# Attention and channel mixing on one core: how the first batch's q and k rows reach their tiles, and what TensorE does meanwhile

## The chip, the cores and the metric

The kernel runs on one core of a Trainium2 chip. TensorE (PE) multiplies, VectorE (DVE) copies and reduces, ScalarE (ACT) computes Exp and Ln, GpSimd (POOL) works on SBUF, SyncE (SP) issues DMAs. ACT and POOL can issue DMAs as well. The metric is the device time of one execution in microseconds; the time before is the median of three runs, 1013.5 us (1011.57 to 1015.29).

## The reference

The input x is [16, 512, 128] in float32. With 16 heads, q and k of 8 columns a head and v of 64, the reference computes

```
xn   = layernorm(x)                                    # no affine part
q, k = xn @ Wq, xn @ Wk ;  v = xn @ Wv                 # 16 heads
attn = softmax(causal(q @ k.T / sqrt(8))) @ v @ Wo
prev = xn shifted by one row
xr, xk = mu_r*xn + (1-mu_r)*prev, mu_k*xn + (1-mu_k)*prev
ffn  = sigmoid(xr @ W_r.T) * (relu(xk @ W_k.T)**2 @ W_v.T)
out  = x + attn + ffn
```

## The kernel before

Each batch element is one batch of 20 units. A unit belongs to a group g of two head pairs (four groups a batch) and has a kind t of 0 to 4; `ROWS` and `KEYS` say which 128-row blocks of which pair it covers.

Softmax is done twice over. First `rowscores` computes scores with rows on partitions into one of two `sm` tiles in PSUM, `rowmask` adds the causal mask as a matmul, `rowmax` reduces on DVE (negm<-sm), and `rowsum` takes Exp on ACT with a running sum (sm<-sm,negm). After a group's five units `log_sums` takes Ln, `sub_logs` subtracts, `turn_stats` transposes the result on PE (pm) and splits it into mh and ml, and `put_stats` writes them as two extra rows into the q tile by DMAs from POOL (q<-mh, q<-ml). Then `scores` computes the transposed scores with these rows included (sT<-q,k), so that one Exp (`weights`, e<-sT) gives the final softmax weights. `weigh` multiplies them with v (av), `project_out` applies Wo (po).

The first half runs `LEAD` = 10 units ahead of the second. `unit_work(n)` issues rowscores of unit n+11, scores of unit n, the mask and maximum of n+11, rowsum of unit n+10, `weights` of n, then the pieces that `at(n, f, ...)` has registered for this n, and last turn_stats. Units -11 to -1 are called the lead here: they have no second half. Every engine works in the written order (`_InOrder`); an instruction that waits holds all behind it on its engine.

float32 q and k are split into two float32r parts, hi and lo, so that the scores can run in the faster form. A tile `qs[i]` or `ks[i]` holds, for each of the eight pairs, 32 rows per head (q: hi, lo, hi, lo; k: hi, lo, lo, hi; 8 rows each), one row of ones or zeros and two rows for the statistics; u picks one head of the pair, at partition 64u. The projection leaves hi and lo with (d, head) on partitions, so `project_qk` writes them to DRAM (q two blocks, k three) and `spread_qk` reads them back, 16 rows per DMA, in the new layout. For batch 0 the spreads come in three steps, pairs 0 and 1, 2 and 3, and 4 to 7 (lines 624 to 626 and 647 to 648). The writes of k of batch 0 and its first spreads go through ACT's queue, all others through SP's.

Until unit -1, `m_tile` hands out PSUM tiles in turn from three banks (m, av, sT); a projection needs its bank's last reader to be done. `product` is two matmuls side by side, each for 64 columns; the trace counts two instructions for each.

Before the lead the kernel loads x of batches 0 and 1 and the weights, computes batch 0's layernorm, transposes xn (xnTp), projects q and k, prepares the masks, turns the three ffn weights on PE (wt), then does the layernorm, the transpose and q of batch 1 (lines 638 to 644). Inside the lead come k of batch 1, all eight v products of batch 0 (two of its halves for each of four row blocks, copied out by DVE), the mixes and ffn_r.

Of the kernel before, what the change touches and what calls it, by code (L numbers as in the profile page):

```python
# [17 lines left out]
P = 128  # L18
# [31 lines left out]
def attn_ffn_kernel(  # L50
# [66 lines left out]
    ffn_n = []  # L117
    for i, w in enumerate((W_r, W_k, W_v)):
        t = one.tile([P, D], FP, tag=f"ffn_n{i}", name=f"ffn_n{i}")
        nc.scalar.dma_start(out=t, in_=w)  # L120
        ffn_n.append(t)
    wo = const.tile([P, NPAIR, D], FP, tag="wo", name="wo")
    nc.scalar.dma_start(out=wo, in_=Wo.rearrange("(m p) d -> p m d", p=P))
# [28 lines left out]
    def m_tile(name):  # L152
        n = lent[0] % 3 if lent else 0
        if lent:
            lent[0] += 1
        if n == 1:
            return ps_av.tile([P, T], FP, tag="av", name=name)
        if n == 2:
            return ps_st.tile([P, 2, 512], FP, tag="sT", name=name)[:, 0, :]
        return ps_m.tile([P, 512], FP, tag="m", name=name)  # L160

# [56 lines left out]
    def project_qk(b, is_k, queue=sp):  # L218

        w, name = (wk, "k") if is_k else (wq, "q")  # L220
        pq = m_tile(f"p{name}_{b}")
        product(pq, w, xnTs[b][:, 1 : T + 1])
        hi = one.tile([P, T], FR, tag=f"{name}h", name=f"{name}h_{b}")
        lo = one.tile([P, T], FR, tag=f"{name}l", name=f"{name}l_{b}")
        dve.tensor_copy(hi, pq)
        dve.tensor_tensor(lo, pq, hi.bitcast(FP), ALU.subtract)

        blocks = (hi, lo, hi) if is_k else (hi, lo)
        d = dram.tile([len(blocks), P, T], FP, tag=name, name=f"{name}_{b}")
        for n, half in enumerate(blocks):  # L230
            queue.dma_start(out=d[n], in_=half.bitcast(FP))
        halves[b, name] = d.rearrange("n (d p u) t -> u (n d) p t", u=2, d=DK)

    def spread_qk(b, is_k, m, u, pairs, queue=sp):

        to, name = ((ks if is_k else qs)[b % 2].bitcast(FP), "k" if is_k else "q")
        first = DK * m if is_k else 0
        queue.dma_start(
            out=to[64 * u + 16 * m : 64 * u + 16 * m + 16, pairs],
            in_=halves[b, name][u][first : first + 16, pairs],  # L240
        )
# [3 lines left out]
    def project_v(b, j, i):  # L245
# [4 lines left out]
        dve.tensor_copy(vs[b][:, j, i * 512 : (i + 1) * 512], pv)  # L250
# [341 lines left out]
    make_qk(0)  # L592
    for c in range(NB):
        row_moments(0, c)
# [4 lines left out]
    project_qk(0, False)  # L599
    project_qk(0, True, act)  # L600
# [23 lines left out]
    for pairs in (slice(0, 2), slice(2, 4)):  # L624
        for is_k, m, u in SPREAD:
            spread_qk(0, is_k, m, u, pairs, act if is_k and pairs.stop == 2 else sp)

    ffn_w = const.tile([P, 3, D], FP, tag="ffn_w", name="ffn_w")
    wt = m_tile("wt")
    for i in range(3):  # L630
        pe.transpose(wt[:, i * D : (i + 1) * D], ffn_n[i], ident)
    dve.tensor_copy(ffn_w.rearrange("p i d -> p (i d)"), wt[:, 0 : 3 * D])

# [3 lines left out]
    load_x(2)  # L637
    for c in range(NB):
        row_moments(1, c)
    deviation(1)  # L640
    for c in range(NB):
        normalise(1, c, dve)
    transpose_xn(1)
    project_qk(1, False)
    first = -LEAD
    at(first + 1, project_qk, 1, True)
    for m, part in enumerate(SPREAD):
        at(first + 2 + m // 2, spread_qk, 0, *part, slice(4, NPAIR))
    for m, n in enumerate((0, 2, 3, 4, 5, 6, 7, 9)):
        at(first + n, project_v, 0, m // 2, m % 2)  # L650
    for i in range(2):
        at(first - 1 + 5 * i, mix_prev, 0, i)
        at(first + 1 + 6 * i, mix, 0, i)
# [47 lines left out]
```

## Time and profile before

| what | value |
|---|---|
| median of the runs | 1013.5 us |
| the profiled execution's own time | 1015.34 us |
| span of its trace | 1013.6 us |
| busy: PE, ACT, DVE, POOL | 949.4, 921.6, 790.4, 512.4 us |
| first softmax Exp on ACT | 29.41 us |
| first Exp of transposed scores | 58.39 us |
| mean granted TensorE clock | 0.975 |

The profile follows one execution. Busy time is the union of an engine's instructions; a granted clock of 1.00 is full, 0.50 is half speed. A group's row gives the line, the engine, the operation, the tiles out<-in, and the count. The chain of waits is followed back from the last instruction: each piece is what released the next. Queue rows (SPq, ACTq) show when a DMA was issued, not when it landed. Nearly every instruction stands under one helper line (L44), so rows are told apart by their tiles.

### The profile page before, as it was taken

The numbers are of one execution on the slowest core, as the hardware profiler recorded it, in microseconds if no ns is written. First come the engines' busy times: TensorE is split into PE (matmuls) and PEld (weight loads), VectorE is DVE, ScalarE is ACT, GpSimd is POOL, SyncE is SP. The second block draws the span as 40 slices with busy tenths as digits, with TensorE's granted clock in tenths as the row PEclk, the third lists the DMA queues.
The fourth block names the chain that finished last, engine by engine and source line by source line (L and its number), as shares of the span: only waits on it lengthen the run. The fifth ranks groups of instructions, "written<-read, shape, count | busy, mean of one in ns | idle before, by whom it ended". The sixth has DMA issues, their size and how long they took to land.

```text
span 1013.6 us, 22825 instructions
## 1 busy us (share of the span) xinstructions
PE 949.4 (94%) x8131; PEld 524.4 (52%) x8131; DVE 790.4 (78%) x1312; ACT 921.6 (91%) x2449; POOL 512.4 (51%) x959
## 2 busy tenths in 40 slices
PE   3888999999999999999999999999999999999997
PEld 1244464555546455554645555464555646455454
DVE  4777878787887878788787878878787887877641
ACT  0688999999999999999999999999999999999982
POOL 4146364554646455454645555464465546434431
PEclk8578999999999999999999999999999999999999
DMA  8730513535142353514235341423534131343000
GB/s 183 134 45 13 110 19 70 91 70 91 34 101 28 70 91 70 90 34 99 31 70 90 70 91 34 96 34 70 90 71 81 33 95 25 70 80 49 3 13 11
DMA packets 59968, 67.10 MB, mean 66 GB/s; under 512 B 12928, under 2 KB 33024, under 8 KB 59856
## 3 DMA queue, kind: packets, MB, share of 16 engines
q1 hardware_dynamic: 48688, 61.89, 32.4%
q10 hardware_dynamic: 2528, 2.43, 1.0%
q0 software_dynamic: 8640, 1.34, 1.0%
q8 instruction: 65, 1.06, 0.5%
q14 instruction: 47, 0.39, 0.1%
HBM read 39.13 MB, written 25.17 MB: 63 GB/s over the span
## 4 chain that ended last, share of the span: by engine, by line
ACT 55%; PE 27%; issue 8%; DVE 7%; DMA 2%; POOL 1%; ACTq 0%; POOLq 0%
ACT sm L44 37%; ACT e L44 17%; PE av L44 9%; PE po L44 5%; DVE negm L44 4%; PE sm L44 4%; PE pv L44 3%; PE sT L44 3%; PE xnTp L44 1%; PE pr L44 1%; DVE xnT L44 1%; DMA q<-ml 1%; DVE v L44 1%; DMA k<-k 1%; PE pk L44 1%
## 5 line engine op out<-in xcount | busy, mean ns | idle before, releaser
L44 ACT ACTIVATE sm<-sm,negm 128x384 f32<-128x384 f32 (+3 forms) x1024 | 513.0, 501 | 64.9 <-DMA k<-k 27.3
L44 DVE TENSOR_REDUCE negm<-sm 128x2 f32<-128x768 f32 (+3 forms) x448 | 397.9, 912 | 101.3 <-PE sm L44 99.2
L44 POOL TENSOR_SCALAR_AFFINE_SELECT e<-e 128x256 f32<-128x256 f32 x512 | 200.5, 410 | 432.4 <-ACT e L44 432.3
L44 PE MATMUL av<-e,v 128*64 128x512 f32 (+3 forms) x2048 | 336.5, 438 | 2.4 <-DVE ctx L44 2.4
L44 ACT ACTIVATE e<-sT 128x1024 f32<-128x1024 f32 x320 | 324.1, 1013 | 14.1 <-PE sT L44 14.1
L44 PEld LDWEIGHTS av<-e,v 128*64 128x64 f32 x2048 | 139.7, 137 | 161.6 <-issue 129.6
L44 ACT ACTIVATION_READ_ACCUMULATOR sm<-sm,negm 128x1 f32 x1024 | 200.5, 196 | 0.0
L44 PE MATMUL sm<-k,q 33*128 33x384 f32 (+3 forms) x1024 | 164.8, 378 | 7.4 <-ACT sm L44 5.4
L44 PE MATMUL sT<-q,k 35*128 35x512 f32 (+3 forms) x1024 | 147.7, 335 | 16.5 <-ACT e L44 13.0
L44 PEld LDWEIGHTS sm<-k,q 33*128 33x128 f32 x1024 | 83.6, 188 | 151.8 <-ACT e L44 82.0
L44 PE MATMUL pv<-wv,xnT 128*64 128x512 f32 x512 | 142.3, 633 | 12.6 <-DVE kl L44 5.8
L44 PE MATMUL po<-wo,ctx 128*64 128x128 f32 x2048 | 133.2, 277 | 2.9 <-DVE ctx L44 1.6
L44 PEld LDWEIGHTS po<-wo,ctx 128*64 128x64 f32 x2048 | 109.8, 137 | 15.4 <-DVE v L44 2.6
L44 PEld LDWEIGHTS sT<-q,k 35*128 35x128 f32 x1024 | 91.2, 187 | 45.9 <-ACT e L44 40.0
L44 DVE COPY v<-pv 128x512 f32<-128x512 f32 x128 | 87.6, 684 | 23.2 <-PE pv L44 19.7
L44 DVE COPY ctx<-av 128x512 f32<-128x512 f32 x128 | 87.1, 680 | 12.7 <-PE av L44 12.6
L44 PE MATMUL sm<-mask,id 64*128 64x256 bf16 (+1 forms) x640 | 91.0, 265 | 0.0
L44 POOL DMA_DIRECT2D q<-mh x128 | 69.8, 548 | 24.9 <-DVE mh L44 12.8
L44 POOL DMA_DIRECT2D q<-ml x128 | 65.8, 519 | 0.0
L44 DVE RECIPROCAL sig<-e_sig 128x128 f32<-128x128 f32 x64 | 60.1, 940 | 0.0
L44 POOL TENSOR_SCALAR prev<-xnT,omm 128x512 f32<-128x512 f32 x32 | 50.0, 1564 | 16.2 <-DVE xmix L44 16.2
L44 PEld LDWEIGHTS <-id 64*128 64x128 bf16 x640 | 36.3, 95 | 24.8 <-issue 10.5
(63 smaller groups left out, 571.1 us busy)
## 6 DMA issues: line engine op xcount, KB each, us to landing
q<-q SPq DMA_DIRECT2D x124, 128.0 KB, 4.9
k<-k SPq DMA_DIRECT2D x124, 128.0 KB, 4.7
k<-kh SPq DMA_DIRECT2D x30, 256.0 KB, 2.6
x<-in_L_attn_x_dram SPq DMA_DIRECT2D x16, 256.0 KB, 6.5
q<-qh SPq DMA_DIRECT2D x16, 256.0 KB, 2.0
q<-ql SPq DMA_DIRECT2D x16, 256.0 KB, 2.1
out_dram<-o SPq DMA_DIRECT2D x16, 256.0 KB, 2.8
k<-kl SPq DMA_DIRECT2D x15, 256.0 KB, 2.0
```

The lines of the kernel that those rows point to most:

```text
L44: return self._tc.keep_in_program_order(f(*args, **kwargs))
```

## The change

Five things change, all before or inside the lead.

1. `keep_awake(n)` issues n transposes of the identity into one `m_tile` that nobody reads: 32 after `make_qk(0)`, 4 between the transpose of xn and the projection of q.
2. For pairs 0 and 1 of batch 0 the rows are no longer read back from DRAM. `spread_near` copies them from the hi and lo tiles in SBUF straight into the q and k tiles, 8 partitions of 2 KB per DMA, 16 DMAs on SP for q and 16 on ACT for k, issued ahead of the writes to DRAM. The writes all go through SP now; pairs 2 to 7 still come from DRAM.
3. The first five v products of batch 0 are issued right after k, ahead of the first rowscores, and copied out by ACT. Three remain in the lead, at units -9, -8 and -3.
4. The layernorm of batch 1, its transpose and its q move into the lead, k to a later unit of it; its normalise runs on POOL, not on DVE.
5. The ffn weights are loaded by SP after the projections and turned inside the lead; Wo is loaded at unit -3, x of batch 2 at unit -5. The two mixes of batch 0 move by a few units.

```diff
--- before.py
+++ after.py
@@ -114,13 +114,6 @@
         wqk_n.append(t)
     wv = const.tile([P, H * DV], FP, tag="wv", name="wv")
     nc.scalar.dma_start(out=wv, in_=Wv)
-    ffn_n = []
-    for i, w in enumerate((W_r, W_k, W_v)):
-        t = one.tile([P, D], FP, tag=f"ffn_n{i}", name=f"ffn_n{i}")
-        nc.scalar.dma_start(out=t, in_=w)
-        ffn_n.append(t)
-    wo = const.tile([P, NPAIR, D], FP, tag="wo", name="wo")
-    nc.scalar.dma_start(out=wo, in_=Wo.rearrange("(m p) d -> p m d", p=P))
     if B > 1:
         load_x(1)
     mus = const.tile([P, 2], FP, tag="mus", name="mus")
@@ -158,6 +151,12 @@
         if n == 2:
             return ps_st.tile([P, 2, 512], FP, tag="sT", name=name)[:, 0, :]
         return ps_m.tile([P, 512], FP, tag="m", name=name)
+
+    def keep_awake(n):
+
+        pt = m_tile("awake")
+        for c in range(n):
+            pe.transpose(pt[:, (c % NB) * P : (c % NB + 1) * P], ident, ident)
 
     xnTs, vs, ctxs, ffns, xmix = {}, {}, {}, {}, {}
 
@@ -215,7 +214,7 @@
         dve.tensor_copy(xnT[:, 1 : T + 1], pt)
         xnTs[b] = xnT
 
-    def project_qk(b, is_k, queue=sp):
+    def project_qk(b, is_k, first=None):
 
         w, name = (wk, "k") if is_k else (wq, "q")
         pq = m_tile(f"p{name}_{b}")
@@ -227,27 +226,38 @@
 
         blocks = (hi, lo, hi) if is_k else (hi, lo)
         d = dram.tile([len(blocks), P, T], FP, tag=name, name=f"{name}_{b}")
+        if first:
+            first(hi, lo)
         for n, half in enumerate(blocks):
-            queue.dma_start(out=d[n], in_=half.bitcast(FP))
+            sp.dma_start(out=d[n], in_=half.bitcast(FP))
         halves[b, name] = d.rearrange("n (d p u) t -> u (n d) p t", u=2, d=DK)
 
-    def spread_qk(b, is_k, m, u, pairs, queue=sp):
+    def spread_near(is_k, p, half, n, queue):
+
+        to = (ks if is_k else qs)[0].bitcast(FP)
+        half = half.bitcast(FP).rearrange("(d h) t -> h d t", d=DK)
+        for m in ((0, 3), (1, 2))[n] if is_k else (n, n + 2):
+            for u in range(2):
+                row = 64 * u + DK * m
+                queue.dma_start(out=to[row : row + DK, p], in_=half[2 * p + u])
+
+    def spread_qk(b, is_k, m, u, pairs):
 
         to, name = ((ks if is_k else qs)[b % 2].bitcast(FP), "k" if is_k else "q")
         first = DK * m if is_k else 0
-        queue.dma_start(
+        sp.dma_start(
             out=to[64 * u + 16 * m : 64 * u + 16 * m + 16, pairs],
             in_=halves[b, name][u][first : first + 16, pairs],
         )
 
     SPREAD = [(is_k, m, u) for m in range(2) for is_k in (False, True) for u in range(2)]
 
-    def project_v(b, j, i):
+    def project_v(b, j, i, copy=dve.tensor_copy):
         if j == 0 and i == 0:
             vs[b] = big.tile([P, NB, H * DV], FP, tag="v", name=f"v_{b}")
         pv = m_tile(f"pv_{b}_{j}_{i}")
         product(pv, xnTs[b][:, 1 + j * P : 1 + (j + 1) * P], wv[:, i * 512 : (i + 1) * 512])
-        dve.tensor_copy(vs[b][:, j, i * 512 : (i + 1) * 512], pv)
+        copy(vs[b][:, j, i * 512 : (i + 1) * 512], pv)
 
     def mix_prev(b, i):
         prev = one.tile([P, T], FP, tag="prev", name=f"prev_{b}_{i}")
@@ -590,14 +600,18 @@
 
 
     make_qk(0)
+    keep_awake(32)
     for c in range(NB):
         row_moments(0, c)
     deviation(0)
     for c in range(NB):
         normalise(0, c, dve)
     transpose_xn(0)
-    project_qk(0, False)
-    project_qk(0, True, act)
+    keep_awake(4)
+    project_qk(0, False, lambda *both: [spread_near(False, p, half, n, sp) for p in range(2) for n, half in enumerate(both)])
+    project_qk(0, True, lambda *both: [spread_near(True, p, half, n, act) for p in range(2) for n, half in enumerate(both)])
+    for m in range(5):
+        project_v(0, m // 2, m % 2, act.copy)
 
 
 
@@ -621,36 +635,48 @@
             dve.tensor_copy(to[half], wide[half, i, P * u : P * u + P])
 
     make_qk(1)
-    for pairs in (slice(0, 2), slice(2, 4)):
-        for is_k, m, u in SPREAD:
-            spread_qk(0, is_k, m, u, pairs, act if is_k and pairs.stop == 2 else sp)
-
-    ffn_w = const.tile([P, 3, D], FP, tag="ffn_w", name="ffn_w")
-    wt = m_tile("wt")
-    for i in range(3):
-        pe.transpose(wt[:, i * D : (i + 1) * D], ffn_n[i], ident)
-    dve.tensor_copy(ffn_w.rearrange("p i d -> p (i d)"), wt[:, 0 : 3 * D])
-
+    ffn_n = []
+    for i, w in enumerate((W_r, W_k, W_v)):
+        t = one.tile([P, D], FP, tag=f"ffn_n{i}", name=f"ffn_n{i}")
+        sp.dma_start(out=t, in_=w)
+        ffn_n.append(t)
+    for part in SPREAD:
+        spread_qk(0, *part, slice(2, 4))
 
     omm = const.tile([P, 2], FP, tag="omm", name="omm")
     dve.tensor_scalar(omm, mus, -1.0, 1.0, ALU.mult, ALU.add)
-    load_x(2)
+
+    ffn_w = const.tile([P, 3, D], FP, tag="ffn_w", name="ffn_w")
+    wo = const.tile([P, NPAIR, D], FP, tag="wo", name="wo")
+
+    def turn_ffn():
+        wt = m_tile("wt")
+        for i in range(3):
+            pe.transpose(wt[:, i * D : (i + 1) * D], ffn_n[i], ident)
+        dve.tensor_copy(ffn_w.rearrange("p i d -> p (i d)"), wt[:, 0 : 3 * D])
+
+    def load_wo():
+        sp.dma_start(out=wo, in_=Wo.rearrange("(m p) d -> p m d", p=P))
+
+    first = -LEAD
     for c in range(NB):
-        row_moments(1, c)
-    deviation(1)
+        at(first - 1 + c // 2, row_moments, 1, c)
+    at(first + 1, deviation, 1)
     for c in range(NB):
-        normalise(1, c, dve)
-    transpose_xn(1)
-    project_qk(1, False)
-    first = -LEAD
-    at(first + 1, project_qk, 1, True)
+        at(first + 1 + c // 2, normalise, 1, c)
+    at(first + 3, transpose_xn, 1)
+    at(first + 4, project_qk, 1, False)
+    at(first + 5, turn_ffn)
+    at(first + 6, project_qk, 1, True)
+    at(first + 5, load_x, 2)
+    at(first + 7, load_wo)
     for m, part in enumerate(SPREAD):
         at(first + 2 + m // 2, spread_qk, 0, *part, slice(4, NPAIR))
-    for m, n in enumerate((0, 2, 3, 4, 5, 6, 7, 9)):
+    for m, n in ((5, 1), (6, 2), (7, 7)):
         at(first + n, project_v, 0, m // 2, m % 2)
     for i in range(2):
-        at(first - 1 + 5 * i, mix_prev, 0, i)
-        at(first + 1 + 6 * i, mix, 0, i)
+        at(first + 2 + 4 * i, mix_prev, 0, i)
+        at(first + 4 + 4 * i, mix, 0, i)
     at(first + 8, ffn_r, 0)
     at(first + 9, ffn_exp, 0)
     for c, n in enumerate((1, 2, 3, 3)):
```

## The prediction

> **What bounds the kernel now.** I read the clock and busy rows of the page first, then a table of stages, then the chain of waits and the timeline of the first 60 us.
>
> ```profile
> PE   3888999999999999999999999999999999999997
> ACT  0688999999999999999999999999999999999982
> PEclk8578999999999999999999999999999999999999
> ```
>
> After the third slice (76 us) PE and ACT are full in every slice. The page's slices are too coarse for the start, so I cut it where ACT's work changes: first softmax Exp at 29.41, first Exp of transposed scores (e) at 58.39, twentieth unit after it at 125.16, and one whole batch. Columns: stretch, length, PE, PEld, DVE, ACT, POOL, granted clock, DMA share, GB/s.
>
> ```profile
> 2.07:29.41 27.34, 11.67 (x37) 4.49 (x37) 14.30 (x45) 0.00 (x1) 10.68 (x20) 0.77 0.94 195
> 29.41:58.39 28.98, 24.10 (x107) 8.41 (x103) 21.30 (x31) 22.62 (x76) 5.22 (x6) 0.68 0.84 128
> 58.39:125.16 66.77, 59.84 (x405) 29.22 (x406) 54.25 (x87) 58.19 (x154) 36.22 (x62) 0.87 0.21 45
> 125.16:184.47 59.31, 57.62 (x511) 32.40 (x508) 48.81 (x82) 57.35 (x154) 31.82 (x59) 1.00 0.34 67
> ```
>
> A batch costs 59.31 us with ACT busy 57.35, and the change leaves that alone. To be won are ACT's 27.34 us of idleness before its first Exp (A), 28.98 - 22.62 = 6.4 us idle in the lead (B), and 66.77 - 59.31 = 7.5 us in the first twenty units (C). The chain says who holds ACT in A and B:
>
> ```profile
> 13.96 0.70 DVE kh L44
> 14.69 0.70 DVE kl L44
> 15.41 4.88 DMA k<-kl
> ...
> 21.62 5.02 DMA k<-k
> 26.66 2.77 DMA k<-k
> 29.43 0.67 ACT sm L44 x2
> ...
> 32.85 1.90 PE pk L44 x4
> ...
> 35.61 1.90 PE pv L44 x4
> ...
> 48.36 8.96 DMA q<-ml
> 57.32 0.14 issue
> 57.46 0.57 PE sT L44 x2
> ```
>
> In A it is the trip of k through DRAM: 15.41 to 29.43, 14 us. In B it is PE at half clock, with projections between the scores, then q<-ml (the row statistics put into q), which lands as the first e is due. Two rows show what the clock is worth and one how SP issues:
>
> ```profile
> 44.03 1.97 PE L44 MATMUL pv<-wv,xnT 128*64 128x512 f32 x4
> 49.00 1.08 PE L44 MATMUL pv<-wv,xnT 128*64 128x512 f32 x4
> 44.99 1.33 SPq L44 DMA_DIRECT2D q<-q  x2
> ```
>
> The same product takes 1.97 us before 47.8 and 1.08 after. SP issues only two DMAs per 2.05 us there (42.94, 44.99, 47.04): each names one of eight semaphores in turn, shared with ACT, and waits until the DMA eight before it has landed.
>
> **The change, stage A.** Thirty-two transposes of the identity start at 1.85, when POOL has made it. Two transposes of xn stand 0.213 us apart at half clock, so they end by 8.7; xn's first is due at 8.33 but its last waits for DVE until 9.09: at most 0.2 us late, taken as 0. Four more (0.44 to 0.85) fall into PE's 0.79 us gap before pq: 0.
>
> Do these transposes lift the clock? No row shows transposes alone. In 10.25 to 13.67 PE streamed pq and pk for 3.32 of 3.42 us, and at 13.84 three transposes came 0.11 apart, at full clock. By that row 6.8 us of back-to-back transposes do it too; pq and pk then take 1.06 each instead of 1.90, and kl is ready at about 14.3, not 15.38. If not, A is 1.1 later. I take the lift, with 1.1 kept for the range.
>
> One rule speaks against it: the Trainium skill, TensorE: Matmul & The Clock Gate, section on the PE-mode transpose, says transposes do not count as PE activity and full clock does not engage for them. By it the sum would be 1010.1, against 1009.0; no run here shows which holds.
>
> The row copies replace the DRAM trip. For pairs 0 and 1, q's halves go in 16 DMAs on SP (from 12.2), k's in 16 on ACT (from 13.6), 8 partitions and 16 KB each. ACT and SP issue the old 64 KB spreads 0.33 to 0.45 apart: alone, ACT would be through at 13.6 + 16 x 0.44 = 20.6, at 0.33 at 18.9. With eight in flight and the shortest spread's 2.06 us to landing plus a little, one leaves per 0.275; 32 plus q's two writes of 256 KB take 34 x 0.275 = 9.4, so 21.6. The other end is the spacing at which the contended 64 KB spreads landed, 0.53: 34 x 0.53 = 18, so 30.2. A near DMA has a quarter of those bytes and the eight-partition form of the statistics DMAs, which landed in 1.6 at best; I take 21.0.
>
> This delay matters, because the five early v products stand on PE ahead of the first rowscores, and ACT copies them out behind its 16 issues. Three PSUM banks rotate: pv0 to pv2 run by about 15.5, pv3 waits for ACT's first copy. A copy is costed at the 0.65 of ACT's 128x512 Exp: pv3 starts at 21.7. PE has then idled 6 us; after 13.67 it worked 0.72 in 3.41 and the clock fell at 17.08. So pv3 and pv4 cost 1.90 each, to 25.5; rowscores and mask 1.03 (31.82 to 32.85), the two reductions 1.3: first Exp at 27.9, a gain of 1.5. At the ends: 18.9 + 0.65 + 2.1 + 0.7 + 1.3 = 23.7, and 30.2 + 6.9 = 37.1. The copies add 5 x 0.65 to ACT where it is idle; a table load, should Copy need its own, would add 1.28 twice, but Exp and Ln share one, so 0.
>
> SP is passed by 16 issues ahead of the q and k writes, so d is full later, near 25, and pairs 2 and 3 land about 33; they are due at the sixth unit, about 38. The ffn weights moved to SP (three, 64 KB) and wo are due after 40: 0. DVE's 5 x 0.69 of v copies leave it.
>
> **Stage B.** Off PE: five v products, 9.5 us at half clock. Onto it: four transposes 0.85, pq 1.90, wt 0.55; net -6.2. DVE: -3.45, and xnT 0.69, q's halves 1.38, ffn_w 0.56, batch 1's moments 1.4: +0.6. POOL takes the normalise, 4 x 0.79 and the 1.05 of rstd, into a stage where it is busy 5.22 of 28.98: 0; without cover unit -7's transposes hold PE for up to 1.
>
> What remains is the two sm buffers: unit m+2's scores wait for ACT's end of unit m, then need 1.03 on PE, 1.24 on DVE, and hand-offs, about 2.4, while ACT fills only 1.6 with a unit of two 512-wide rows. That is 0.8 at four units, 3.2; with full clock 0.45 each. I keep 1.8 of today's other stalls, since fewer products still stand between scores on PE and DVE is as full: 22.6 + 5.0 = 27.6, gain 1.4. Ends: 22.6 + 1.8 = 24.4; today's plus DVE's, 29.6.
>
> The first e comes at 27.9 + 27.6 = 55.5. It also needs q<-ml: lz came 12.8 after the first Exp, POOL's first issue 5.1 after that, its second pair 1.1 later, 8.96 to landing: 55.8. Queued around it now are k's 768 KB and wo's 512 KB, while batch 1's spreads, which ran ahead there, wait behind them; undisturbed it took 1.6. On the edge: 0.
>
> **Stage C.** No instruction in it changes. Two half-clock spells lie in it, 58.04 to 68.28 and 88.76 to 95.58; the chain's PE pieces in them (sT 0.79, pk 1.90, av 1.71, sm 0.72, sT 0.43; then sT 0.86, pv 1.90, av 2.56) would halve, 2.8 and 2.7. The first followed PE's idling for q<-ml (1.21 busy in 54.62 to 58.04). I count about half of one: 1.6; ends +5.5 and, with one more such spell, -2.7.
>
> **Sum.** 1.5 + 1.4 + 1.6 = 4.5 us. The profiled execution took 1015.3 (span 1013.6 and 1.7 around it), 1.8 above the median of 1013.5; it becomes 1010.8, and on the median 1009.0.
>
> **Rivals.** *Small DMAs clog (slower).* ACT sits behind its 16 issues, PE behind pv3. For: the spreads landed 0.53 apart, eight in flight. Against: a quarter of the bytes. From 0.36 us per DMA on, A eats B's and C's gains; at 0.5 it ends at 36.1: +6.7 - 3.0, 1017.2.
>
> *Statistics take it back (no change).* q<-ml needs 12 instead of 9 because of wo and k: first e at 58.8, PE idles, the clock falls, A and B gain nothing: 1013. Against: the spreads that crowded it are later.
>
> *The clock holds (more).* Sustained PE work from pv3 on lifts it for the lead: A 25.5, B 24.4, C 62: 3.9 + 4.6 + 4.8 = 13.3, 1000.2. For: pv3 to the second unit's scores are 5.5 us without a gap. Against: 34.15 to 47.8 was nearly gapless on PE and stayed at half clock.
>
> **How the numbers follow.** Forecast 0.50 (own range 1005 to 1013), clock 0.18, statistics 0.20, clog 0.12. 0.3% is 3.0 us, about what a measurement of this kernel can tell. Faster: 0.40 of the forecast, all 0.18, 0.02 of the statistics: 0.60. Slower: 0.09 of the clog and 0.03 of the statistics: 0.12. Same: 0.28. The range 1002.0 to 1016.0 leaves out about half of the clock case and half of the clog.
>
> **What would show it.** Transposes 0.11 apart before 8 us: the lift. ACT's last near issue at 21.0 and pv3 right after ACT's first copy: the wait I add. First Exp at 27.9, first e at 55.5, twentieth unit at 120.7. pv in the lead at 1.97: half clock. It is wrong if near DMAs leave faster than 0.2 or slower than 0.36 apart, if pv3 does not wait for ACT, or if batches after the second no longer take 59.3.

## The result and the profile after

The changed kernel takes 1018.7 us (median of six executions, 1016.03 to 1020.12) against 1012.8 for the kernel before (six executions, 1009.48 to 1015.29): a ratio of 1.0058, 95% interval 1.0035 to 1.0082. It is slower by 5.9 us where 4.5 faster was forecast. The profiled execution took 1016.03 us (span 1014.3).

The page's rows for PE, ACT and the granted clock, in 40 slices, look as before: only the first four slices differ.

```profile
PE   4788999999999999999999999999999999999997
ACT  0688999999999999999999999999999999999982
PEclk8769999999999999999999999999999999999999
```

The table of stages of the changed kernel, cut at the same events as before (first softmax Exp at 32.81, first e at 61.15, twentieth unit after it at 125.61, one batch). Columns: stretch, length, busy time and count of PE, PEld, DVE, ACT and POOL, granted clock, DMA share, GB/s.

```profile
2.07:32.81 30.74, 16.86 (x78) 9.21 (x77) 8.64 (x28) 2.74 (x6) 7.98 (x17) 0.78 0.51 136
32.81:61.15 28.34, 21.73 (x99) 9.48 (x99) 23.16 (x42) 22.57 (x76) 10.99 (x13) 0.65 0.66 143
61.15:125.61 64.46, 57.40 (x403) 28.48 (x405) 52.68 (x85) 58.24 (x154) 36.26 (x62) 0.92 0.30 59
125.61:184.95 59.34, 57.60 (x511) 32.40 (x508) 49.05 (x82) 57.41 (x155) 31.79 (x59) 1.00 0.37 67
```

A batch still costs 59.3. The clock of stage A is too high in both tables: the profile counts the time ahead of its first clock record as full. That record begins at 6.91 here, and until then the transposes stood 0.213 apart, 0.11 after it. Stage A is longer by 3.4 us, although its DMA share fell from 0.94 to 0.51: the engines that move data are no longer what it waits for. The timeline of the stage shows what is. Columns: start, busy time, engine (SPq and ACTq are DMA issues), operation, tiles, count, and in brackets the idle time before it with what ended it.

```profile
12.02 3.72 SPq L44 DMA_DIRECT2D q<-qh  x4
13.35 4.39 ACTq L44 DMA_DIRECT2D k<-kh  x4
15.85 3.53 SPq L44 DMA_DIRECT2D q<-ql  x4
17.84 2.64 ACTq L44 DMA_DIRECT2D k<-kl  x4
...
20.52 2.92 ACTq L44 DMA_DIRECT2D k<-kh  x4
...
23.48 2.92 ACTq L44 DMA_DIRECT2D k<-kl  x4
...
26.45 1.56 ACT L44 COPY v<-pv 128x512 f32<-128x512 f32 x3 [24.38 <-DMA k<-kl]
...
27.09 3.68 PE L44 MATMUL pv<-wv,xnT 128*64 128x512 f32 x8 [11.81 <-ACT v L44]
...
30.70 0.54 PE L44 MATMUL sm<-k,q 33*128 33x384 f32 x4
...
32.81 0.56 ACT L44 ACTIVATE sm<-sm,negm 128x384 f32<-128x384 f32 x1 [1.42 <-DVE negm L44]
```

ACT issues its sixteen near copies from 13.35 to 26.40; four take 2.92 there, 0.73 each. Its first copy of v starts at 26.45, and PE, idle for 11.81 us, starts the fourth v product when ACT's copy is out. The bracket names a DMA, but ACT's own queue ended at 26.40 (23.48 + 2.92): the copy came right behind the last issue. From there it is the chain that the prediction wrote down, 6.4 us long, only 5.4 us late.

Two windows of the same execution, 12.0 to 17.2 and 17.2 to 24.0, same columns, say the rest:

```profile
12.00:17.20 5.20, 3.03 (x14) 0.54 (x10) 2.77 (x8) 0.00 (x0) 0.00 (x0) 1.00 0.37 40
17.20:24.00 6.80, 0.00 (x0) 0.00 (x0) 0.00 (x0) 0.00 (x0) 0.00 (x0) 0.50 0.12 40
```

In the second, no engine computes anything and the DMA engines are 12% busy, with the copies that SP and ACT issue.

Each kernel was traced three times. Stages, in us:

| | A, to first Exp | B, to first e | C, twenty units | end of C |
|---|---|---|---|---|
| before | 29.41, 29.22, 29.43 | 28.98, 27.79, 27.16 | 66.77, 67.17, 65.18 | 125.16, 124.19, 121.77 |
| after | 32.81, 32.83, 33.07 | 28.33, 28.32, 29.21 | 64.47, 64.44, 64.66 | 125.61, 125.59, 126.94 |

A grew by 3.55 on average and by at least 3.4 whichever traces are compared; that is fixed. B is 0.6 longer on average and C 1.85 shorter, but before's own C moved by 2 between executions, so neither is settled by three traces. Behind the end of C all six traces take 888.1 to 889.2. The mean of the ends differs by 2.3, the medians of the times by 5.9: 3.6 of the loss is in no trace. The three traced executions of the changed kernel took 1016.03, 1015.43 and 1016.81; those that were only timed went up to 1020.12. Each came with a mean granted clock: 0.978 for 1016.03, 0.974 and 0.975 for 1017.27 and 1017.42, 0.970 for the three at 1020.0 to 1020.12. Among the executions of this one program the longer ones are those with the lower clock. That the clock makes them longer, and where in the execution it would, no run shows. The kernel before can't be set beside these figures: its 126 executions timed beside the experiments had 0.973 to 0.995, but its clock records begin at 13.66 in the first trace and at 36.21 in the second, what lies ahead counts as full, and yet pq took 1.97 and 1.98 there, as at half clock. The second trace has a mean of 0.990 and took 1014.93.

### The profile page after: what moved, and what is told of

It is laid out like the page before. It is cut to its first block, busy times and chain, and to the rows that moved or that the text cites. A ratio compares the mean times of both kernels' runs of the same rounds, so it can differ in the third digit from the quotient of the medians.

```text
span 1014.3 us, 22931 instructions
## 1 busy us (share of the span) xinstructions
PE 950.0 (94%) x8167; PEld 529.4 (52%) x8167; DVE 784.6 (77%) x1303; ACT 925.0 (91%) x2454; POOL 515.8 (51%) x963
## 3 DMA queue, kind: packets, MB, share of 16 engines
q8 instruction: 65, 1.06, 0.5%
## 4 chain that ended last, share of the span: by engine, by line
ACT 62%; PE 21%; issue 9%; DVE 5%; DMA 1%; ACTq 1%; POOL 0%; POOLq 0%
ACT sm L44 42%; ACT e L44 19%; PE av L44 7%; PE po L44 4%; PE pv L44 3%; PE sm L44 3%; DVE negm L44 3%; PE sT L44 3%; PE xnTp L44 1%; ACT e_sig L44 1%; ACTq L44 1%; DMA q<-qh 1%; DVE xnT L44 0%; PE pk L44 0%; DVE ctx L44 0%
## 5 line engine op out<-in xcount | busy, mean ns | idle before, releaser
L44 PE MATMUL pv<-wv,xnT 128*64 128x512 f32 x512 | 141.3, 631 | 24.6 <-ACT v L44 11.8
L44 DVE COPY v<-pv 128x512 f32<-128x512 f32 x123 | 84.2, 685 | 22.0 <-PE pv L44 18.3
L44 PEld LDWEIGHTS pv<-wv,xnT 128*64 128x64 f32 x512 | 28.6, 138 | 39.1 <-PE sm L44 16.3
```

What stands on the lines that cost most here:

```text
L44: return self._tc.keep_in_program_order(f(*args, **kwargs))
```

## The experiments

Theory: stage A is set by the time that a queue needs to issue a near copy, passed on one for one through ACT's copies of v and the products behind them. Rivals that came up on the way: the copies wait for the DMA engines, which batch 1's fills of constant rows occupy; the clock is what keeps stage B long. "A" is the first softmax Exp in the trace; each median stands beside that of the kernel before in the same series.

### DVE instead of ACT copies the early v

```diff
-        project_v(0, m // 2, m % 2, act.copy)
+        project_v(0, m // 2, m % 2)
```

> The changed kernel with one edit: the five early v products are copied out of PSUM by DVE instead of ACT. Theory (queue): the wait added by the change is PE's pv3 behind ACT's first copy behind ACT's 16 near issues (first copy 26.45, pv3 27.09). Then pv3 and pv4 run by 17, the first rowscores start when the rows of pair 0 have landed (its last k piece landed near 21.2 in the changed kernel's trace), and the first Exp moves from 32.8 to 26.5, held only by ACT's own issues, which end at 26.4; the time falls by about 6 us against the changed kernel, to about 1012.5, level with the kernel before. Rival (landing): the rows themselves come late; then the first Exp stays at 31 or later and the time within 2 us of the changed kernel's 1018.7.

Measured: 1011.1 (12 executions) against 1012.0, ratio 0.9997 (0.9986 to 1.0009); A 26.85, B 29.4, C 64.8. The timeline:

```profile
23.52 1.29 DVE L44 TENSOR_REDUCE negm<-sm 128x2 f32<-128x768 f32 x2 [4.93 <-PE sm L44]
23.77 2.97 ACTq L44 DMA_DIRECT2D k<-kl  x4
...
26.85 0.56 ACT L44 ACTIVATE sm<-sm,negm 128x384 f32<-128x384 f32 x1 [24.77 <-DMA k<-kl]
```

This edit returns 6 us of stage A: PE no longer waits for ACT. The first maximum is ready at 24.8, and ACT still can't begin, because its own queue holds it until 26.74. So the wait is ACT's sixteen issues, through its v copies in the changed kernel and directly here.

### Without the near copies

Pairs 0 and 1 come from DRAM as before, k's writes and first spreads go through ACT, the rest of the change stays.

```diff
-    project_qk(0, False, lambda *both: [spread_near(False, p, half, n, sp) for p in range(2) for n, half in enumerate(both)])
-    project_qk(0, True, lambda *both: [spread_near(True, p, half, n, act) for p in range(2) for n, half in enumerate(both)])
+    project_qk(0, False)
+    project_qk(0, True, queue=act)
...
+    for is_k, m, u in SPREAD:
+        spread_qk(0, is_k, m, u, slice(0, 2), act if is_k else sp)
```

> The changed kernel without its near copies: pairs 0 and 1 come from DRAM again, with k's writes and first spreads on ACT's queue as in the kernel before; the transposes of the identity, the early v products, batch 1's work in the lead all stay. Theory (queue): ACT issues 3 writes and then copies, so its first copy comes near 15 and pv4 ends near 19; the first rowscores wait for the spreads and start near 25; first Exp near 28, 5 us earlier than in the changed kernel; time about 1014. Rival (the work moved into the lead is what costs): first Exp near 28 as well, but the lead grows past 30 us and the time stays above 1017.

Measured: 1013.4 (10) against 1012.0, ratio 1.0016 (1.0001 to 1.003); A 29.56, B 28.09, C 64.39. A is that of the kernel before. k's first write goes out at 13.35 instead of 14.69, but ACT issues k's first spreads behind its copies of v, at 20.91 instead of 20.31; whether they could have gone earlier was not tested. With A unchanged, the moves of stages B and C, from which 3.0 us were forecast, show no gain: 1.6 slower (0.1 to 3.0). Two series of one program can differ by as much, as DVE's copies do below (0.9997 here, 0.9981 there).

### Without the identity transposes

```diff
-    keep_awake(32)
...
-    keep_awake(4)
```

> The changed kernel without the 36 transposes of the identity. In the changed kernel's trace the clock rises at 6.9, during the transposes, and pq and pk take 1.08 and 1.03 instead of 1.97 and 1.80. Theory (the transposes do lift the clock but it is lost again by 17): without them pq and pk run at half clock, the near issues start about 1.1 later and so does the first Exp, at 33.9; time up by about 1, 1019.7. Rival (the transposes gain nothing since ACT's issues hold all): first Exp within 0.3 of 32.8, time the same. Rival (they cost): first Exp earlier than 32.5.

Measured: 1017.1 (4) against 1012.0, ratio 1.0058 (1.0043 to 1.0073); A 33.54, C 64.67. The projections with the transposes (the changed kernel) and, in the second fence, without them:

```profile
10.18 1.08 PE L44 MATMUL pq<-xnT,wq 128*64 128x512 f32 x4 [0.35 <-DVE xnT L44]
...
11.09 1.03 PE L44 MATMUL pk<-xnT,wk 128*64 128x512 f32 x4
```

```profile
10.43 1.98 PE L44 MATMUL pq<-xnT,wq 128*64 128x512 f32 x4 [0.79 <-DVE xnT L44]
...
12.19 1.92 PE L44 MATMUL pk<-xnT,wk 128*64 128x512 f32 x4
```

The lift is real. k's first near copy goes out at 13.35 instead of 14.88, but the gain in A is only 0.7 us, because the issue time behind it stays, and the ratio, 1.0058 with and without the transposes, doesn't show it.

### All near copies on SP

```diff
-    project_qk(0, True, lambda *both: [spread_near(True, p, half, n, act) for p in range(2) for n, half in enumerate(both)])
+    project_qk(0, True, lambda *both: [spread_near(True, p, half, n, sp) for p in range(2) for n, half in enumerate(both)])
```

> The changed kernel with all 32 near copies issued by SP, none by ACT. In the changed kernel each queue needs about 0.74 per near copy while both issue, 0.37 together. If what limits is shared by both queues (0.37 each), SP is through near 25, k's pair 0 has landed near 22.5 and the first Exp comes near 25, as ACT's copies now start at 14; time about 1011. If each queue needs 0.7 for one of these DMAs by itself, SP issues q's 16 until 23.5 and k's pair 0 until 30, the first Exp comes near 34 and the time is 1019 or more.

Measured: 1017.2 (4) against 1012.0, ratio 1.0061 (1.0043 to 1.0079); A 33.06, B 27.45, C 66.8. SP's issues, alone on their way:

```profile
18.20 2.39 SPq L44 DMA_DIRECT2D q<-qh  x4
...
24.08 2.43 SPq L44 DMA_DIRECT2D k<-kh  x4
...
26.61 2.39 SPq L44 DMA_DIRECT2D k<-kl  x4
```

Four take 2.39, and with the gap behind them one leaves per 0.61; the old spreads of 16 partitions leave this queue 0.47 apart. With SP and ACT at work together it is 0.74 on each, one per 0.37 over both. A copy has landed when the last event of its semaphore comes: 1.86 after its issue begins when SP is alone, 2.24 with ACT beside it. So three are in flight, or six over both queues, and the limit of eight that the prediction reckoned with does not bind. It did once, in the stall ahead: in the changed kernel the first copy landed only at 17.15, and ACT's fourth, the ninth of both queues, began at 17.17.

### Near copies for one pair only, and more transposes in the lead

Pair 1 comes from DRAM, the writes to DRAM stand ahead of the near copies, k's on ACT, and DVE copies v; the second version adds 36 transposes of the identity behind the early v products and 2 to 9 in each lead unit (the last three lines).

```diff
+        for n, half in enumerate(blocks):
+            queue.dma_start(out=d[n], in_=half.bitcast(FP))
         if first:
             first(hi, lo)
-        for n, half in enumerate(blocks):
-            sp.dma_start(out=d[n], in_=half.bitcast(FP))
...
-    project_qk(0, False, lambda *both: [spread_near(False, p, half, n, sp) for p in range(2) for n, half in enumerate(both)])
-    project_qk(0, True, lambda *both: [spread_near(True, p, half, n, act) for p in range(2) for n, half in enumerate(both)])
+    project_qk(0, False, lambda *both: [spread_near(False, p, half, n, sp) for p in range(1) for n, half in enumerate(both)])
+    project_qk(0, True, lambda *both: [spread_near(True, p, half, n, act) for p in range(1) for n, half in enumerate(both)], act)
...
+    for part in SPREAD:
+        spread_qk(0, *part, slice(1, 2))
...
+    keep_awake(36)
...
+    for n, m in enumerate((9, 9, 2, 2, 5, 2, 5, 2, 2, 2, 8)):
+        at(first - 1 + n, keep_awake, m)
```

> The changed kernel with DVE's copies of the early v products, near copies for pair 0 alone (8 on SP, 8 on ACT) behind the writes to DRAM instead of ahead of them, k's writes on ACT, and pair 1 read back from DRAM like pairs 2 and 3. Theory (each near copy costs a queue 0.6 to 0.74 of issue, and ACT's first Exp waits for ACT's last one): ACT's last near issue moves from 26.4 to about 21.7, the first Exp from 26.85 (with DVE's copies alone) to about 25.0; time about 1009, 2 below the kernel before. Rival (the lead takes it back, as PE stays at half clock in it): first Exp near 25 but the first e later than 55, time 1011 as with DVE's copies alone.

> The kernel of e7_pair0 with more transposes of the identity: 36 after the early v products, and 2 to 9 at the end of every unit of the lead. Theory (the lead is held by PE at half clock): the granted clock stays at 1.00 from about 7 us on, the lead falls from 29 to about 25, first e near 50, time about 1005. Rival (ACT, DVE and the two score buffers hold the lead at any clock): clock at 1.00 but the lead within 1 us of that of e7_pair0. Rival (they stand in the way): lead longer than with e7_pair0.

Measured: 1013.3 (12) and 1014.9 (12) against 1013.4, ratios 1.0003 (0.9992 to 1.0015) and 1.0023 (1.0009 to 1.0038); A 28.72 and 28.44. In the first the writes ahead of them pushed ACT's near copies back to 18.68, so halving their number gained nothing. The windows of stage B, without the extra transposes and, in the second fence, with them:

```profile
28.72:57.93 29.21, 24.10 (x99) 10.64 (x99) 23.24 (x42) 22.57 (x75) 10.99 (x13) 0.50 0.67 154
```

```profile
28.44:58.62 30.18, 25.94 (x146) 14.21 (x144) 23.23 (x42) 22.70 (x75) 10.98 (x13) 0.78 0.64 141
```

The clock rises from 0.50 to 0.78 and the lead is 1 us longer, not shorter. But the fence counts 47 more instructions on PE, which stand between the scores, so this run can't tell a clock that is worth nothing from transposes that take back what it gives.

### The transposes alone, in the kernel before

```diff
+    keep_awake(32)
...
+    keep_awake(4)
...
+    keep_awake(50)
...
+    keep_awake(16)
```

(behind batch 0's tiles, ahead of its q, behind its k, behind batch 1's q)

> The kernel before with transposes of the identity alone: 32 at the start, 4 before pq, 50 after batch 0's k, 16 after batch 1's q; nothing else of the change. Theory (lead held by PE at half clock): first Exp about 28.3 (pq and pk at full clock), lead about 25 to 26, time about 1008, 4 below the kernel before. Rival: clock at 1.00 in the lead but the lead above 28; time within 1 of the kernel before, or above it where the 50 transposes hold up batch 1's xn.

Measured: 1015.2 (12) against 1013.4, ratio 1.0022 (1.001 to 1.0034); A 31.47, B 27.95, C 67.27. The last 16 transposes run from 26.51 to 29.49, at half clock again, and the first rowscores start at 29.41 behind them: that is the 2 us of A. Like the run before, this one prices transposes that stand in the way and not the clock.

### A third queue, and batch 1's fills

k's near copies of pair 1 go through POOL, DVE copies v, and the block that builds masks stands ahead of the projections. The second version adds the last two lines, which issue the mixes at units -5 and -3.

```diff
-    project_qk(0, True, lambda *both: [spread_near(True, p, half, n, act) for p in range(2) for n, half in enumerate(both)])
+    project_qk(0, True, lambda *both: [spread_near(True, p, half, n, pool if p else act) for p in range(2) for n, half in enumerate(both)])
...
-        at(first + 4 + 4 * i, mix, 0, i)
+        at(first + 5 + 2 * i, mix, 0, i)
```

> The changed kernel with DVE's copies of the early v products and with k's near copies for pair 1 issued by POOL instead of ACT (the block that makes id2 and mask2 stands ahead of the projections, so that it isn't behind POOL's copies); ACT issues 8 near copies, SP 16, POOL 8. Theory (near copies cost their queue's issue time, and ACT's Exp waits for ACT's): ACT is through near 20.5 instead of 26.7, the first rowscores start near 21 as with DVE's copies alone, and the first Exp follows PE and DVE at about 24, 3 us earlier than with DVE's copies alone; time about 1008, 4 below the kernel before. Rival (the rows of pair 1, needed two units later, now bind): first Exp near 24 but the third unit's scores wait, first e within 1 us of 56.2, time 1011.

> The kernel of e10_pool_queue with batch 0's first mix at unit -5 instead of -6, where DVE has q's two halves to make (with DVE's copies alone, ACT idled 1.46 us there behind qh, ql and xmix). Theory (DVE's clump holds the maximum): that gap falls by about 0.7 and the lead by 0.5 to 1; time 0 to 1 below e10_pool_queue. Rival: the gap moves to the next unit, lead unchanged within 0.3.

Measured: 1015.1 (12) and 1013.8 (12) against 1012.8, ratios 1.0021 (1.0007 to 1.0034) and 1.0012 (1.0001 to 1.0023); A 29.6 and 29.29, longer than with two queues and DVE copies. One issue of ACT and one of SP took 4.46 and 3.69, at 19.5 and 20.3, just when POOL issued its next DMAs: four that fill the constant rows of batch 1's q and k tiles. In the changed kernel POOL issues them at 9.60 to 11.91, and there the first near copy took 5.1 us to land. So the fills were suspected. Two versions wrote them later, at unit -11, on top of the DVE copies and of the second version here:

```diff
-    make_qk(1)
...
+    at(first - 1, make_qk, 1)
```

> The kernel of e1_dve_copy (the changed kernel with DVE's copies of the early v products) with batch 1's eight fill rows of q and k, four DMAs from POOL, moved from ahead of the near copies (issued 9.6 to 11.9) to the first unit of the lead. Theory (the fills hold the DMA engines): in the changed kernel the first near copy took 5.1 us to land (12.02 to 17.15) and ACT's fourth issue waited for it until 17.17; without the fills it lands in 2, ACT's last issue ends near 25.2 instead of 26.7, the first rowscores start near 20 instead of 21.7, the first Exp near 25.3 instead of 26.85; time 1 to 1.5 below e1_dve_copy, 1009.8. Rival (the stall has another cause): ACT's fourth issue again near 17.2, first Exp 26.8.

> The kernel of e11_pool_mix (k's near copies for pair 1 on POOL, first mix a unit later) with batch 1's fills moved to the first unit of the lead. In e10_pool_queue and e11_pool_mix, where the fills stood behind POOL's near copies, one issue on ACT took 4.46 us at 19.48 and one on SP 3.69 at 20.25. Theory (fills hold the engines): both return to 0.75 or less, ACT is through near 19.5, the first Exp comes near 23, first e near 52, time about 1008, 4 below the kernel before. Rival (three queues at once cost more per issue): ACT's issues above 0.8 each, first Exp above 25.

Measured: 1010.9 (12) and 1014.1 (12) against 1013.6, ratios 0.9981 (0.9969 to 0.9994) and 1.001 (0.9995 to 1.0024). They tell nothing of the fills: nothing ahead of them on POOL waits, so they went out at 9.6 and at 18.0 as before. The first is a second measurement of DVE's copies (A 26.74). The second shows the collision once more:

```profile
15.86 2.14 POOL L44 DMA_DIRECT2D k<-kl  x4
...
17.06 7.07 ACTq L44 DMA_DIRECT2D k<-kl  x4
...
17.39 6.99 SPq L44 DMA_DIRECT2D q<-qh  x4
18.00 0.54 POOL L44 DMA_DIRECT2D q<-fill  x1
```

To move them, they (four DMAs, though an expectation below says ten) were written behind batch 1's transpose, where POOL's normalise stands ahead of them: once with near copies on two queues, once on three.

```diff
-    make_qk(1)
...
+    at(first + 3, make_qk, 1)
```

> DVE copies the early v out, as in the first experiment, and the ten fills of batch 1's q and k tiles are written behind batch 1's transpose, so that POOL issues them behind its normalise, at some 38 us, and not at 9.6 to 11.9. Theory: the fills hold the DMA engines when the first near copies start. Then the first near copy lands in about 2 us instead of 5.1, ACT's fourth near issue is not held to 17.2, ACT's last is through by about 24.5, the first Exp comes at about 25.3 (26.85 and 26.74 in the two versions before) and the time is some 1.2 us below theirs, about 1009.8. Rival: the stall has another cause (the first copies of q's rows of 2 KB from 8 partitions, or x of batch 1 on the queues); then the first copy takes 5 us again, the first Exp stays at 26.7 to 26.9 and the time at 1011.

> k's near copies of pair 1 on POOL's queue, DVE copies the early v out, the mixes at units -5 and -3, and the fills of batch 1's tiles behind batch 1's transpose. In the two versions before it, the fills were issued at 18.0 to 20.4 right behind POOL's near copies, and an issue of ACT and one of SP at 19.4 to 20.3 took 3.7 to 4.8 us. Theory: the fills do it. Then no near issue takes over 1.5 us after 18, ACT is through with its 8 near issues by about 20, the first Exp comes at about 25 (29.2 to 29.6 before) and the time falls by about 3.5 us to some 1010. Rival: the queues hold each other up with 48 near copies and writes, whatever the fills do: an issue of 3.5 us or more stays, the first Exp stays above 28 and the time at 1013 to 1014.

Measured: 1011.2 (11) and 1010.5 (6) against 1013.4, ratios 0.9983 (0.9975 to 0.9992) and 0.9966 (0.9954 to 0.9978); A 25.92 and 25.89. The fills went out at 37.3 to 39.9. Two queues, then in the second fence three:

```profile
12.13 2.54 SPq L44 DMA_DIRECT2D q<-qh  x4
13.46 3.54 ACTq L44 DMA_DIRECT2D k<-kh  x4
14.77 2.58 SPq L44 DMA_DIRECT2D q<-ql  x4
```

```profile
17.86 2.14 POOL L44 DMA_DIRECT2D k<-kl  x4
...
18.61 3.05 ACTq L44 DMA_DIRECT2D k<-kl  x4
18.96 3.25 SPq L44 DMA_DIRECT2D q<-qh  x4
```

The first copy lands after 1.96 us instead of 5.13, SP's first four need 2.54 instead of 3.72, and no near issue on three queues takes over 1.2. The DMA share between 12.0 and 17.2 falls from 0.41 (with DVE copies and early fills) to 0.09. So the fills cause both stalls. With two queues that is worth only 0.9 us of stage A, because the sixteen issues on ACT, now 0.78 apart, still last until 25.8; that version's time is no better than the 0.9981 of the one with early fills. With three queues the gain was 3.4 us in A and, by the ratios, 4.7 us in time; A there includes 1.9 us that are not the queues': a weight arrived 1.0 late in that execution (wk<-wk_n at 6.03, 5.0 to 5.1 in the others), the clock, full from 4.76, fell at 11.59, pq and pk took 1.66 and 1.93, and k's first near copy left at 15.35 instead of 13.4 to 13.5. Its chain shows what a copy takes to land, from the start of ACT's last issue:

```profile
20.93 2.33 DMA k<-kl
```

### Three queues, the first pair first

On top of the last: k's copies are dealt out by head over ACT and POOL, pair 0 first, and q's last four are split between them.

```diff
+    def near_k(*both):
+        for p in range(2):
+            for n, half in enumerate(both):
+                spread_near(True, p, half, n, (act, pool))
+        spread_near(False, 1, late[0], 1, (act, pool))
...
-                queue.dma_start(out=to[row : row + DK, p], in_=half[2 * p + u])
+                queues[u].dma_start(out=to[row : row + DK, p], in_=half[2 * p + u])
```

> The version with near copies on three queues and late fills, with k's copies dealt out by head over ACT and POOL, pair 0 first, and the last four of q's given to both at the end (10, 10 and 12 issues in place of 8, 8 and 16). Theory: the first two units need pair 0 alone, and ACT's eight copies of k's pair 0 (last landing 22.37) held the first row scores until 22.59, while q's pair 0 had landed at 19.63. With four on each queue pair 0 is all in at 18.5 to 20, the first Exp comes at 22 to 23.5 (25.89 before) and the time is 1 to 2.5 us under the 1010.5 of the version before, if the second unit's successors do not wait for pair 1. Rival: three queues that issue at once cost more per issue (over 0.9 us), or the third unit waits for pair 1 and the lead takes back what stage A gains: time within 0.7 us of 1010.5.

Measured: 1009.0 (6) against 1013.2, ratio 0.9947 (0.9929 to 0.9965). This version is faster than both kernels. Of the 4.1 us that its A is below that of the version before, 1.9 are that version's late start. Its stages, and the row of the first Exp:

```profile
2.07:21.79 19.72, 15.36 (x78) 9.27 (x77) 11.89 (x34) 0.01 (x2) 11.16 (x23) 0.94 0.45 117
21.79:51.05 29.26, 23.73 (x99) 9.97 (x99) 22.89 (x42) 22.67 (x75) 13.29 (x17) 0.56 0.82 195
51.05:117.36 66.31, 59.59 (x403) 29.14 (x405) 52.69 (x85) 58.25 (x154) 36.34 (x62) 0.88 0.30 61
```

```profile
21.79 0.56 ACT L44 ACTIVATE sm<-sm,negm 128x384 f32<-128x384 f32 x1 [19.71 <-DMA k<-kl]
```

A is 7.6 us shorter than before's, the time 5.4 (3.5 to 7.2) by the ratio. PE keeps its clock until 19.50 and loses it then (0.56 in the lead); C, with a clock of 0.88, holds 1.8 us more than in the changed kernel.

### Both kernels traced again

> The kernel before, unchanged, profiled once more. The two traces differ by 0.7 us in span where the medians differ by 5.9. Theory (the trace of before was one of its slower executions, with 53 us at half clock): another execution shows a higher mean granted clock than 0.975 and the first Exp at 29.4 again, but a lead below 28.98 and a shorter stretch after it. Rival: first Exp, lead and stretch within 0.3 of the first trace, and the difference lies behind the first two batches.

> The changed kernel, unchanged, profiled once more: its first trace came from the fastest of its six executions (1016.0; median 1018.7). Theory (the first Exp is fixed by issue times and the rest by the phase of the clock): first Exp within 0.5 of 32.8 again, lead or the stretch after it longer than 28.3 and 64.5 by the 2 to 4 us that this execution takes more, with more half clock in the records. Rival: the first Exp itself varies by more than 1 us.

> The kernel before, profiled a third time: its two traces have spans of 1013.6 and 1013.2, where its median execution has 1010.2. Theory (the phase of the clock's windows against the start makes the difference): where this execution's span is below 1011, the lead is below 27.5 or the stretch of twenty units after it below 66, with A at 29.3 again.

> The changed kernel, profiled a third time: its two traces have spans of 1014.3 and 1013.7, where its median execution has 1017.0. Theory (phase of the clock's windows): where this execution's span is above 1016, the first Exp is still within 0.5 of 32.8, and lead or the stretch after it is longer, with more time at half clock.

Their stages stand in the table of the first section; the times were 1014.93 and 1012.67 for the kernel before, 1015.43 and 1016.81 for the changed one. Before's first trace, on which the prediction rests, was one of its longer executions: its stages B and C held 1.8 and 1.6 us more than the third's.

These traces bear on stage B as well. Below are the lead of the changed kernel's third trace, and lead and stage C of the version with all near copies on SP, whose lead is written the same:

```profile
33.07:62.28 29.21, 22.86 (x99) 9.92 (x99) 23.41 (x42) 22.55 (x75) 10.98 (x13) 0.56 0.63 135
33.06:60.52 27.46, 17.57 (x99) 8.02 (x99) 23.13 (x42) 22.55 (x76) 10.98 (x13) 0.81 0.82 189
60.52:127.32 66.80, 60.89 (x403) 29.68 (x405) 52.39 (x84) 58.26 (x155) 36.26 (x62) 0.85 0.28 58
```

The changed kernel's own lead took 28.3 at 0.64 and 0.65 and 29.2 at 0.56; here it takes 27.5 at 0.81. So the clock does go with the length of the lead, by up to 1.8 us. In the versions with the mixes moved the lead stayed at 28.8 to 29.3, at clocks from 0.50 to 0.68. What this lead gained was lost again in C, which took 66.8 at 0.85 against 64.5 at 0.92.

## Why the prediction was wrong

**Where the 10.4 us lie.** The forecast was 4.5 faster, the result 5.9 slower. Over the three traces of each kernel stage A holds 5.0 of it (27.9 forecast, 32.9 measured), stage B 1.0 (27.6 and 28.6) and stage C -0.7 (65.2 and 64.5). Another 1.5 is the choice of the start: the sum began from the first trace of the kernel before, whose stage C ends 1.5 later than the mean of the three. The third has a B of 27.16 and a C of 65.18 without any change, so the gains of 1.4 and 1.6 lie within what that kernel varies by. The last 3.6 are in no trace.

**The price of a near DMA: the step that failed.** The sum took 0.275 us per copy over both queues, from eight in flight and 2.06 us to landing. The runs show 0.37: 0.74 on each queue, which is issue time. Landing was sized well, at 2.24 (2.06 is the first of the spread's sixteen events; it landed after 2.31): eight in flight would have let one leave per 0.28. It was not the limit that bound. The prediction had the form of the right answer in "alone, ACT would be through at 13.6 + 16 x 0.44", with the row of the 16-partition spread; the near copy costs 0.73 there, and 13.35 + 16 x 0.73 = 25.0. It went below that because a near copy has fewer bytes, and bytes were not what it cost. The fills' stall, priced at nothing, is 0.9 of the 1.4 left up to 26.4, by what A gained when the fills came later. That is ACT 5.4 us later than 21.0, and A 4.9 later than 27.9.

The Trainium skill, DMA: Bandwidth & Descriptors, section "Issuing engines are not separate DMA queues", says that starting DMAs from several engines saves only the sequencer's time to initiate them, "which is usually small relative to the DMA itself". The first half fits: three queues helped just by issue time. Here the second half does not hold: 0.73 of issue stood against 2.24 to landing, a third of it, at a DMA share of 0.12.

**The wait that the change adds: right.** Pv3 began behind ACT's first copy, PE idled 11.8 us before it (6 were forecast), the clock fell at 17.15, and pv3 and pv4 ran at half clock. The chain from ACT's last issue to the first Exp took 6.4 us (6.9 forecast). Moving the copies to DVE, which the prediction did not weigh, removes it.

**The lift by transposes: right.** They stood 0.213 apart, then 0.11 once the clock was granted in full at 6.91 us; pq and pk took 1.08 and 1.03. By 6.91 PE had done nothing but these transposes. So the rule of the Trainium skill, TensorE: Matmul & The Clock Gate, section on the PE-mode transpose, that they do not count as activity, does not hold for this kernel; the measurement decides. The trace lists the transposes as MATMUL and does not say in what mode they run. In the changed kernel the lift was worth 0.7 us of A, with 1.1 reckoned. It can be lost: with three queues and late fills the clock fell at 11.59, during pq.

**Stage B: not gained.** 27.6 was forecast, 28.3, 28.3 and 29.2 came. The products that left it freed PE, and ACT was busy for 22.6 of it as before. Its length goes with the clock, 29.2 at 0.56 and 27.5 at 0.81, but the one run meant to raise the clock, to 0.78, put transposes between the scores and was longer. How much the clock, the two sm buffers and DVE each bind, no run isolated.

**Stage C: 65.2 forecast, 64.4 to 64.7 in the traces.** That looks like more than the gain of 1.6, but the time doesn't have it. With stage A as before, the rest of the change measured 1.6 us slower (0.1 to 3.0), where the sum had 3.0 faster. Why the time doesn't have it stays open: the executions above 1017 were not traced. Over thirteen versions with the change's lead (without the one that has transposes in it, each A from one trace), a straight line through the time differences rises by 1.06 us per us of A and stands at +1.6 for before's A of 29.35: 3.55 x 1.06 + 1.6 = 5.4 of the measured 5.9. These versions differ in more than A, so the line supports the split and does not prove it.

**The rivals.** *Small DMAs clog* came nearest: its threshold was 0.36 us per copy and 0.37 was measured, but the clog is in the queues that issue and not in what is in flight. That the two figures agree is luck. In the prediction's own formula, 12.2 + 34 x price + 6.9, A eats the 3.0 us of B and C only from 0.39 on, and 0.37 gives an A of 31.7; the stall and ACT's place behind its own queue made it 32.8. It had 0.12, too little, since the nearest issue rows (0.33 to 0.45 for larger copies) gave 0.17 to 0.23 over two queues at best and nothing excluded more. *Statistics take it back* did not: q<-ml had landed by 53.7, 7.5 us ahead of the first e. *The clock holds* did not: 0.65 in the lead.

**The range** of 1002 to 1016 left half of the clog out, and the time, 1018.7, fell there, 1.5 us beyond the price of that rival. A's upper end of 37.1 stood in the working, and A came to rest halfway between 27.9 and it; it was given too little.

## What to carry to other kernels

Price a DMA on the queue that issues it and by a row of its own kind: sixteen small copies in front of an engine's next work cost that engine sixteen issue times, however few the bytes. When DMA share is low and queue rows are back to back, deal the copies out over another queue, what is needed first ahead, and give any compute behind them to an engine that issues none. A DMA with nothing due soon (a fill, a prefetch) belongs behind an instruction that holds it back, since moving its line in an in-order queue with no wait ahead moves nothing.

## What the runs showed of the hardware that was not expected

- Issue time depends on the kind of copy and on company: 0.56 us (0.61 apart) for a near copy of 8 partitions on SP alone, 0.70 (0.74 apart) on SP and ACT together, 0.54 on POOL beside both; spreads of 16 partitions from DRAM 0.42, with four times the bytes. Near copies differ from spreads in shape and in source, and no run separates the two.
- Four fills of constant rows (batch 1's q and k tiles) made a near copy, issued just behind them, take 5.1 us instead of 2.0 to land, at a DMA share of 0.37, and held single issues of two other queues for 3.7 to 4.8 us.
- Copies from PSUM by ACT took 0.59 to 0.61 each for 128x512 (0.49 apart in a row), less than the 0.65 of its Exp, and no second table load is in the trace.
- With the same program the mean granted clock of an execution differed between 0.970 and 0.978, and the time by 4 us with it. One kernel with extra transposes spanned 0.976 to 0.990, and 1018.7 to 1013.0.
